# A reordered last stage: output norms on four column tiles, normalised input turned by DMA

## The chip, the cores and the metric

The kernel runs on one core of one Trainium2 chip. The metric is the device time of one launch in microseconds (us), as the median over runs. The engines are named as in the profile: PE (TensorE matmul), PEld (its weight loads), DVE (VectorE), ACT (ScalarE), POOL (GpSimd) and SP (SyncE, which issues most DMAs here).

## The reference, cut to what matters

The model has two layers, each an attention and a feed-forward part, over 16 batches of 256 tokens of width 256. The last part is a gated linear attention. For one batch, `x` being 256 by 256:

```python
xn = layernorm(x)
q1, k1, v = xn @ Wq, xn @ Wk, xn @ Wv          # 8 heads of 64
q2 = xn @ Wqa @ Wqb;  k2 = softmax(xn @ Wka @ Wkb)
gk1, gk2 = log_sigmoid(xn @ Wg1a @ Wg1b) / 16, log_sigmoid(xn @ Wg2a @ Wg2b) / 16
e = softmax(xn @ We);  mask = one_hot(top1(e));  fac = e * mask
o = gla(q1, k1, v, gk1) + sum over experts of gla(q2*fac, k2*fac, v, gk2*mask)
g = xn @ Wga @ Wgb
o = o * rsqrt(mean(o*o over the head's 64 columns) + eps) * norm_w
o = o * (g * sigmoid(g))
x = x + tanh(g_ffn) * (o @ Wo)
```

The change touches how this part is scheduled and, most of all, the line with `rsqrt(mean(o*o))`, which this text calls the output norm: one factor for each token and head, 256 by 8 for a batch.

## The kernel before, in words

The kernel computes everything in float32. Stages 0 to 2 hold the first three parts of the model. The last stage (`stage3_fast`) takes up about the last third of the span and is written as a software pipeline by hand.

The stage's loop `for p in range(last)` runs over 64 steps: `p // 4` is the batch and `p % 4` a pair of heads, so a batch has four steps. A pair's data lie with the 128 columns of two heads over the partitions and the 256 tokens along the free dimension. In every step the same core work is done for one pair:

- `keys_queries(p+1)`: keys and queries of the next step into the PSUM bank `kq` (four 128x256 products).
- `decays(p+1)`: cumulated gate logarithms for the dense part (`gq`, with the mask `dmask`) and the routed part (`gz`, with the mask `em`); ACT makes `ee`, their exponentials.
- `products(p, 0)`: attention scores of the dense part into the PSUM tile `sc`. There is one such tile of two banks, so the next user of `sc` waits until VectorE has read it.
- `masked(p, 0)`: VectorE multiplies `sc` with a mask into `at`. `factors(p+1)`: VectorE makes `f` from `kq` and `ee`.
- `values(p-1)`: `at` of the step before times `v`, into the PSUM bank `o`.
- `second(p+1)`, `factors_second(p+1)`: second half of `gq`, and keys of the routed part for a later batch (`e2`); VectorE makes `q`, POOL makes `k`.
- `products(p, 1)`: scores of the routed part, again into `sc`; in the next step `masked(p, 1)` has VectorE multiply them (four instructions), and POOL add them to `at`.

The rest of a batch's work is hung into these steps by tables (`start`, `copies`, `middle`, `rest`, `late`, `behind_mask`, `by_rows`, `logs`): each maps `p % 4` to a list of functions with a distance in batches. The engines keep the order in which the program issues instructions, each engine for itself, so these tables fix the queues of PE, VectorE, ACT, POOL and SP. The functions that the change and the prediction touch:

- `stats`, `norm_ahead`: mean and variance of `x` (VectorE, then four small POOL instructions), and the normalised `xn` (two ACT instructions), two batches ahead.
- `turn_ahead`: `xn` is turned into `xnT` with 16 VectorE transposes of 32 partitions by 128 columns (a 128-column instruction turns four blocks of 32x32).
- `lows`: PE multiplies `xnT` with the low-rank matrices; VectorE copies them to `low`, and a second time 2x32 rows to `low2`; a DMA makes `lowd`.
- `outgates`: PE makes the gate logits `zg` in two banks; ACT makes `eg = exp(-zg)` and copies `zg` to `zs`.
- `all_gates`: gate logits `z` in two banks, and in the same tile `sc` that the scores use.
- `route`, `turn_hot`, `turned_hot`, `pairs`: the chosen expert of each token, its transpose `hT`, and the masks `em` and `am` from it (`both`).
- `shares`, `shares_end`: softmax denominators of the second keys on four column tiles (`den`: four 32x256 products, each with 32 of the 128 columns of PE), a VectorE transpose and their running maximum `second`.
- `squares`, `gated`, `scaled`, `project`: the squares of `o` (`sq`), `u = o * gate`, the output norm (`ms`: a 128x512 product with the block matrix `halves` for each two pairs, which puts each head's sum on all of its 64 partitions; ACT takes logarithm and exponential into `r`; POOL multiplies), and the output projection.

The VectorE instruction order of `shares_end` and `outgates` matters for what follows, since `masked(p, 1)` comes behind them in the queue.

Of the kernel before, what the change touches and what calls it, by code (L numbers as in the profile page):

```python
# [10 lines left out]
F32 = mybir.dt.float32  # L11
I32 = mybir.dt.int32
AF = mybir.ActivationFunctionType
ALU = mybir.AluOpType
AX = mybir.AxisListType
PSUM = bass.MemoryType.PSUM

P = 128
B, S, D = 16, 256, 256
# [4 lines left out]
V_LN1G, V_LN1B, V_LN2G, V_LN2B, V_QB, V_KB, V_NW, V_ONE, V_GATE, V_N = 0, 2, 4, 6, 8, 10, 12, 13, 14, 18  # L24


def bc(ap, shape, *axes):

    for a in axes:
        ap = ap.unsqueeze(a)  # L30
    return ap.to_broadcast(list(shape))
# [42 lines left out]
def layers(ctx: ExitStack, tc: tile.TileContext, t, out, check):  # L74
    nc = tc.nc
# [10 lines left out]
    xs, cs = [None] * B, [None] * B  # L86
# [132 lines left out]
    def normed(dst, src, mv, rs, p=P, n=2):  # L219
        for i in range(n):  # L220
            act.activation(dst[:, i, :], src[:, i, :], AF.Identity, bias=rs[:p, 1, i:i + 1],
                           scale=rs[:p, 0, i:i + 1])

    def turned_squares(xT, x, portion):

        for n in portion:
            q, r = n // 4 * 32, n % 4 * 32
            dve.transpose(xT[r:r + 32].rearrange("p k (i s) -> p i k s", i=2)[:, :, :, q:q + 32],
                          x[q:q + 32].rearrange("p i (k d) -> p i k d", k=2)[:, :, :, r:r + 32])
# [1389 lines left out]
    def stage3_fast(early_bank):  # L1619

        with ExitStack() as sx:
# [7 lines left out]
            def bank(name):  # L1629
                return pss.tile([P, 512], F32, tag="ps", name=name) if pss else early_bank(name)  # L1630
# [5 lines left out]
            def matmul(*a, **k):  # L1636
                tc.keep_in_program_order(nc.tensor.matmul(*a, **k))  # L1637
# [33 lines left out]

            def norm_ahead(b):
                xn[b] = w0.tile([P, 2, D], F32, tag="xn", name="xn")
                normed(xn[b], xs[b], *mvs.pop(b))

            def turn(b):
                xnT[b] = of(b).tile([P, 2, S], F32, tag="xnT", name="xnT")
# [6 lines left out]
            def turn_ahead(b):  # L1684

                xnT[b] = of(b).tile([P, 2, S], F32, tag="xnT", name="xnT")
                turned_squares(xnT[b], xn[b], range(16))

            def lows(b):

                low[b] = of(b).tile([P, 2, S], F32, tag="low", name="low")
                ps = bank("low")
                for c in range(2):
                    for k in range(2):
                        matmul(ps[:, c * S:(c + 1) * S], la[:, k, c * P:(c + 1) * P], xnT[b][:, k, :],
                                         start=k == 0, stop=k == 1)
                dve3.tensor_copy(low[b][:, 0, :], ps[:, :S])
                dve3.tensor_scalar(low[b][:, 1, :], ps[:, S:], vec[:, V_ONE:V_ONE + 1], None, ALU.add)
                lowd[b] = of(b).tile([P, S], F32, tag="lowd", name="lowd")
                nc.sync.dma_start(out=lowd[b][64:], in_=low[b][:64, 1, :])  # L1700
                if b > 0:
                    for r in range(0, 64, 32):
                        dve3.tensor_scalar(low2[r:r + 32, :], ps[64 + r:96 + r, S + P:],
                                           vec[64 + r:96 + r, V_ONE:V_ONE + 1], None, ALU.add)

            e_, den_, z_ = {}, {}, {}

# [99 lines left out]
            def outgates(b):  # L1807

                gw[b] = w2.tile([P, 4, S], F32, tag="gw", name="gw")
                two = [bank("zg"), bank("zg")]  # L1810
                for i in range(2):
                    for h, (w, x) in enumerate(((lbg[0:64], low[b][0:64, 1, :]), (lbg2[64:], lowd[b][64:]))):
                        m = 2 * i + h
                        matmul(two[h][:, i * S:(i + 1) * S], w[:, m * P:(m + 1) * P], x, start=True, stop=True)
                for h, ps in enumerate(two):
                    e, zs = (w2.tile([P, 512], F32, tag=n, name=n) for n in ("eg", "zs"))
                    act3.activation(e, ps, AF.Exp, scale=-1.0)
                    act3.copy(zs, ps)
                    z_[b, h] = zs, e

            def outgates_end(b, h):
# [55 lines left out]
            def shares_end(b):  # L1877
                ps = z_.pop((b, "den"))
                den = w2.tile([P, 8, 32], F32, tag="dens", name="dens")
                dve3.transpose(den.rearrange("p x j -> p (x j)"), ps[:, :S])  # L1880
                rd[b] = st.tile([P, 8, 2], F32, tag="kden", name="kden")
                flat = rd[b].rearrange("p x j -> p (x j)")
                most = check["second"].rearrange("p (x j) -> p x j", j=2)
                dve3.tensor_tensor(most, most, den[:, :, 0::16], ALU.max)
                dve3.reciprocal(rd[b], den[:, :, 0::16])
                pool3.tensor_tensor(check["rsum"][:, :16], check["rsum"][:, :16], flat, ALU.add)

# [62 lines left out]
            def squares(b, mp):  # L1950
                if mp == 0:
                    u_[b] = w2.tile([P, 4, S], F32, tag="u", name="u")
                    oT[b] = w2.tile([P, 4, S], F32, tag="oT", name="oT")
                ps = o.pop((b, mp))
                sq[b, mp] = w2.tile([P, 512], F32, tag="sq", name="sq")
                act3.activation(sq[b, mp], ps, AF.Square)
                z_[b, mp, "o"] = ps

            def gated(b, mp):
# [3 lines left out]

            def scaled(b, mp, by=pool3, beside=()):
                ps = bank("ms")
                matmul(ps, halves, sq.pop((b, mp)), start=True, stop=True)
                for x in beside:
                    x()
                r = w2.tile([P, 512], F32, tag="r", name="r")
                act3.activation(r, ps, AF.Ln, bias=eps, scale=1.0 / 64,  # L1970
                                     accum_out=check["logs"][:, 2 * b + mp:2 * b + mp + 1])
                act3.activation(r, r, AF.Exp, scale=-0.5)
                by.tensor_tensor(oT[b][:, 2 * mp:2 * mp + 2, :].rearrange("p m s -> p (m s)"),
                                        u_[b][:, 2 * mp:2 * mp + 2, :].rearrange("p m s -> p (m s)"), r, ALU.mult)

            def project(b):
                ps = bank("proj")
# [25 lines left out]
                    matmul(ps, ones, v[B - 1][:, 0, :], start=True, stop=True)  # L2003


            start = {2: [(turn_hot, 1)]}
            copies = {2: [(turned_hot, 1)]}
            middle = {0: [(lows, 1)], 1: [(all_gates, 1)], 2: [(pairs, 1)], 3: [(scaled, 0, 0)]}

            rest = {0: [(bias, 2)], 1: [(route, 1)], 2: [(steepest, 1, 0), (stats, 2)], 3: [(steepest, 1, 1), (turn_ahead, 2)]}  # L2010
            late = {1: [(scaled, -1, 1)], 2: [(project, -1)], 3: [(vals, 1)]}
            behind_mask = {0: [(route_logits, 1)]}
            by_rows = {0: [(outgates, 0)], 1: [(gates_end, 1)]}
            logs = {0: [(route_sums, 1), (outgates_end, 0, 0)], 1: [(outgates_end, 0, 1), (gate_logs, 1, 0)], 2: [(gate_logs, 1, 1), (norm_ahead, 2)]}

            def run(steps, p):
                for f, d, *a in steps.get(p % 4, ()):
                    if 0 <= p // 4 + d < B:
                        f(p // 4 + d, *a)
# [36 lines left out]
            for p in range(last):  # L2056
                if p == 0:
                    turn(1)
                run(start, p)
                if p % 4 == 0:  # L2060
                    shares(p // 4)
                if 0 < p:
                    masked(p - 1, 1)
                run(copies, p)
                if p % 4 == 0:
                    shares_end(p // 4)
                if 1 < p and p % 2 == 1:
                    gated((p - 2) // 4, (p - 2) % 4 // 2)
                if p + 1 < last:
                    keys_queries(p + 1)  # L2070
                run(middle, p)
                run(rest, p)
                if p + 1 < last:
                    decays(p + 1)
                run(late, p)
                products(p, 0)
                masked(p, 0)
                run(behind_mask, p)
                if p + 1 < last:
                    factors(p + 1)  # L2080
                run(by_rows, p)

                inside = p % 4 > 0 and p + 1 < last
                if inside:
                    summed(p)
                if p + 1 < last:
                    second(p + 1)
                    factors_second(p + 1)
                run(logs, p)
                products(p, 1)  # L2090
                if 0 < p and not inside:
                    summed(p)
# [128 lines left out]
```

## Time and profile before

| | us |
|---|---|
| median of 3 runs | 1845.09 |
| the three runs | 1840.51, 1845.09, 1845.21 |
| the profiled execution | 1847.08 |
| span of its profile | 1845.3 |
| mean granted TensorE clock in it | 0.995 |
| one batch of the last stage in its steady state (from one `v` product group to the next) | 37.72 |

The profiled execution took 1.8 us more than the span from its first to its last instruction, and 2.0 us more than the median of the runs. A row of the timeline has the start and the duration in us, the engine, the line (that of a helper for most instructions here, so rows are told apart by their tiles), the operation, the tile written, the tile read, the shape, how many instructions the row merges, and in brackets how long the engine had been idle and who released it. A float32 product appears as two instructions. Matmul ends are modelled, so distances between starts are more to be trusted than durations.

### The profile page before, as it was taken

Reading aid. Unit: us, or ns where it says so; the run is one execution under the profiler, and the core shown is the slowest. Engines: PE = TensorE matmul, PEld = TensorE weight load, DVE = VectorE, ACT = ScalarE, POOL = GpSimd, SP = SyncE. Lnnn points to the kernel's source line nnn. Section 1 sums busy time; section 2 is a strip of 40 time slices with the busy share of each in tenths; the row PEclk is TensorE's granted clock in tenths of the full one; section 3 lists DMA queues with packets and bytes.
Section 4 is the critical chain, followed back from the end, with each engine's and each line's share of the span. In section 5 each row is a group of like instructions: output and inputs, shape, how many; then the busy total and the mean of one; then the engine's idle time right before and its main releaser. Section 6 shows DMA issues by size and latency. Waiting matters only on the chain.

```text
span 1845.3 us, 35182 instructions
## 1 busy us (share of the span) xinstructions
PE 1813.5 (98%) x13870; PEld 1249.8 (68%) x13870; DVE 1231.5 (67%) x2903; ACT 873.9 (47%) x1804; POOL 1017.0 (55%) x1001
## 2 busy tenths in 40 slices
PE   8999999999999999999999999999999999999997
PEld 5666666666766667666777766656767777777765
DVE  3355656566665666656474488867888878878874
ACT  4433344433444334443433487846555645455543
POOL 4654767567676576756634767315444444444433
PEclk9999999999999999999999999999999999999999
DMA  9800010000010100000077933100000000000000
GB/s 304 226 1 22 16 34 15 25 17 23 23 37 8 29 19 10 31 23 18 13 248 238 233 49 49 18 4 3 14 8 10 8 10 13 8 9 8 14 9 14
DMA packets 68504, 85.86 MB, mean 47 GB/s; under 512 B 10740, under 2 KB 55908, under 8 KB 67818
## 3 DMA queue, kind: packets, MB, share of 16 engines
q1 hardware_dynamic: 56041, 66.74, 11.5%
q0 software_dynamic: 12288, 16.79, 4.5%
q8 instruction: 111, 1.82, 0.4%
q14 instruction: 64, 0.52, 0.1%
HBM read 44.17 MB, written 38.29 MB: 45 GB/s over the span
## 4 chain that ended last, share of the span: by engine, by line
PE 82%; POOL 9%; DVE 4%; issue 2%; ACT 2%; DMA 1%; SPq 0%; POOLq 0%; DVEq 0%; ACTq 0%
PE o L50 11%; PE qk L50 11%; PE v L50 8%; PE sc L50 8%; PE proj L50 7%; PE kq L1637 7%; PE sc L1637 5%; POOL es L50 4%; PE gq L1637 3%; PE v L1637 3%; PE o L1637 3%; PE proj L1637 3%; POOL x L50 2%; PE ex L50 2%; POOL rs L50 2%
## 5 line engine op out<-in xcount | busy, mean ns | idle before, releaser
L50 POOL TENSOR_SCALAR rs<-mv 128x2 f32<-128x2 f32 (+2 forms) x85 | 16.3, 192 | 376.8 <-DVE mv L50 371.1
L50 DVE RECIPROCAL rd<-o 128x256 f32<-128x256 f32 x64 | 112.3, 1755 | 164.0 <-PE o L50 123.7
L50 POOL TENSOR_TENSOR at<-at,at 128x768 f32<-128x768 f32 x63 | 114.1, 1812 | 142.4 <-DVE at L50 142.4
L50 ACT ACTIVATE e<-sc 128x1024 f32<-128x1024 f32 (+1 forms) x192 | 181.7, 1016 | 18.4 <-PE sc L50 18.4
L50 PE MATMUL sc<-qk 64*128 64x256 f32 (+1 forms) x1536 | 183.1, 384 | 0.5 <-DVE qk L50 0.5
L50 PE MATMUL o<-e,v 128*32 128x256 f32 (+1 forms) x3072 | 177.9, 379 | 0.0
L50 PEld LDWEIGHTS sc<-qk 64*128 64x128 f32 (+1 forms) x1536 | 132.0, 172 | 55.1 <-issue 26.8
L50 POOL TENSOR_TENSOR esum<-esum,es 128x512 f32<-128x512 f32 x128 | 163.5, 1277 | 10.0
L50 PE MATMUL qk<-kvT,wkv 128*128 128x333 f32 x512 | 164.3, 443 | 0.0
L50 ACT ACTIVATE qk<-qk 128x256 f32<-128x256 f32 x128 | 48.8, 381 | 231.4 <-PE qk L50 231.4
L50 POOL TENSOR_TENSOR es<-e 128x1024 f32<-128x1024 f32 x64 | 151.2, 2363 | 12.1 <-ACT e L50 9.0
L50 POOL TENSOR_TENSOR es<-es,e 77x1024 f32<-77x1024 f32 x64 | 150.4, 2350 | 5.0
L50 PEld LDWEIGHTS o<-e,v 128*32 128x32 f32 (+1 forms) x3072 | 99.9, 110 | 66.3
L50 PE MATMUL qk<-kvT,wq 128*128 128x256 f32 x512 | 134.6, 385 | 0.0
L50 DVE COPY qk<-qk 128x333 f32<-128x333 f32 x128 | 64.6, 504 | 93.8 <-ACT qk L50 92.8
L50 POOL DMA_INDIRECT x<-rows_out,pos x64 | 101.1, 1580 | 33.2 <-issue 17.0
L50 PEld LDWEIGHTS qk<-kvT,wq 128*128 128x128 f32 x512 | 94.3, 189 | 35.2 <-issue 9.6
L50 PEld LDWEIGHTS qk<-kvT,wkv 128*128 128x128 f32 x512 | 97.2, 190 | 30.0
L50 PE MATMUL proj<-wo0h,oT 128*128 128x256 f32 x512 | 113.7, 380 | 0.3 <-DVE oT L50 0.3
L50 PE MATMUL v<-wkv,kvT 128*128 128x512 f32 x256 | 113.1, 595 | 0.0
L50 PEld LDWEIGHTS proj<-wo0h,oT 128*128 128x128 f32 x512 | 95.9, 190 | 13.9 <-issue 0.8
L50 POOL DMA_INDIRECT rows<-xw,pos x64 | 66.8, 1043 | 61.1 <-ACT xT L50 24.0
(265 smaller groups left out, 4085.7 us busy)
## 6 DMA issues: line engine op xcount, KB each, us to landing
rows<-zero SPq DMA_DIRECT2D x16, 640.0 KB
xin<-rows SPq DMA_DIRECT2D x16, 640.0 KB
rows_out<-y SPq DMA_DIRECT2D x16, 384.0 KB
v<-vctx SPq DMA_DIRECT2D x15, 308.0 KB
x<-in_x_dram SPq DMA_DIRECT2D x16, 256.0 KB
rows_out<-y SPq DMA_DIRECT2D x16, 256.0 KB
out_dram<-x SPq DMA_DIRECT2D x15, 256.0 KB
wkv<-in_wkv_dram SPq DMA_DIRECT2D x2, 1024.0 KB
```

The costliest lines, as they stand in the source:

```text
L50: x = getattr(self.engine, name)(*a, **k)
L1637: tc.keep_in_program_order(nc.tensor.matmul(*a, **k))
```

## The change

It does the following in the last stage, for all batches but the last where the output norm is concerned:

- The output norm of a batch is done at once (`norms`) instead of in two halves: four 32x256 products on four column tiles, one for each pair, with 32 columns of `halves`; then one logarithm and one exponential over 128x256; the eight useful rows go to DRAM, and two DMAs bring them back, each row spread over the 64 partitions of its head. POOL's two multiplications (`normed_out`) are later, and in place, as `oT` is now the same tile as `u`.
- `turn_ahead` has one VectorE transpose of 128x512 into a new tile `turned` (32x32 blocks in place), and 16 DMAs on SP's queue, each 32 partitions by 4 pieces of 128 bytes, put the blocks where they belong. `norm_ahead` writes `xn` in an order that suits this.
- `low2` is made by a DMA from `low` in place of two VectorE instructions.
- `outgates`: VectorE copies `zg` to `zs`, where ACT did.
- `shares_end`: the running maximum is a reduction with one operand into a column of its own, where it was a `max` of two tiles.
- The tables are changed, and in the first step of a batch `values` comes before `second`, as in the other three.

```diff
             def norm_ahead(b):
...
-                normed(xn[b], xs[b], *mvs.pop(b))
+                every = "p i (k d) -> p i k d"
+                normed(xn[b].rearrange("p k (i d) -> p i k d", i=2), xs[b].rearrange(every, k=2), *mvs.pop(b))
             def turn_ahead(b):
...
-                turned_squares(xnT[b], xn[b], range(16))
+                y = w1.tile([P, 4, P], F32, tag="turned", name="turned")
+                dve3.transpose(y.rearrange("p x d -> p (x d)"), xn[b].rearrange("p k d -> p (k d)"))
+                to = xnT[b].rearrange("p k (i s) -> p (k i) s", i=2)
+                for q in range(0, P, 32):
+                    for r in range(0, P, 32):
+                        nc.sync.dma_start(out=to[r:r + 32, :, q:q + 32], in_=y[q:q + 32, :, r:r + 32])
             def lows(b):
...
-                    for r in range(0, 64, 32):
-                        dve3.tensor_scalar(low2[r:r + 32, :], ps[64 + r:96 + r, S + P:],
-                                           vec[64 + r:96 + r, V_ONE:V_ONE + 1], None, ALU.add)
+                    nc.sync.dma_start(out=low2, in_=low[b][64:, 1, P:])
             def outgates(b):
...
-                    act3.copy(zs, ps)
+                    dve3.tensor_copy(zs, ps)
             def shares_end(b):
...
-                most = check["second"].rearrange("p (x j) -> p x j", j=2)
-                dve3.tensor_tensor(most, most, den[:, :, 0::16], ALU.max)
+                dve3.tensor_reduce(check["second"][:, b:b + 1], den[:, :, 0::16], AX.XY, ALU.max)
...
+            rms = [tc.dram_tile([8, S], F32, name=f"rms{b}") for b in range(B - 1)]
+            def scaled_first(b):
+                if b == B - 1:
+                    scaled(b, 0)
+            def norms(b):
+                if b == B - 1:
+                    return
+                ps, x = bank("ms"), sq.pop(b)
+                for m in range(4):
+                    matmul(ps[32 * m:32 * m + 32, :S], halves[:, 48:80], x[:, m, :], start=True, stop=True)
+                y = w2.tile([P, S], F32, tag="rs", name="rs")
+                act3.activation(y, ps[:, :S], AF.Ln, bias=eps, scale=1.0 / 64, accum_out=check["logs"][:, 2 * b:2 * b + 1])
+                act3.activation(y, y, AF.Exp, scale=-0.5)
+                nc.sync.dma_start(out=rms[b], in_=y[0:P:16, :])
+                r = z_[b, "r"] = w1.tile([P, 4, S], F32, tag="r", name="r")
+                for j in range(2):
+                    nc.sync.dma_start(out=r[64 * j:64 * j + 64],
+                                      in_=bc(rms[b].rearrange("(m j) s -> j m s", j=2)[j], [64, 4, S], 0))
+            def normed_out(b, mp):
+                if b < B - 1:
+                    x, r = oT[b][:, 2 * mp:2 * mp + 2, :], z_[b, "r"][:, 2 * mp:2 * mp + 2, :]
+                    pool3.tensor_tensor(x, x, r, ALU.mult)
...
-            start = {2: [(turn_hot, 1)]}
-            copies = {2: [(turned_hot, 1)]}
-            middle = {0: [(lows, 1)], 1: [(all_gates, 1)], 2: [(pairs, 1)], 3: [(scaled, 0, 0)]}
-            rest = {0: [(bias, 2)], 1: [(route, 1)], 2: [(steepest, 1, 0), (stats, 2)], 3: [(steepest, 1, 1), (turn_ahead, 2)]}
-            late = {1: [(scaled, -1, 1)], 2: [(project, -1)], 3: [(vals, 1)]}
+            start = {3: [(pairs, 1)]}
+            middle = {0: [(lows, 1)], 1: [(all_gates, 1)], 2: [(turn_hot, 1)], 3: [(scaled_first, 0)]}
+            rest = {0: [(bias, 2)], 2: [(turned_hot, 1), (norm_ahead, 2)], 3: [(steepest, 1, 0), (steepest, 1, 1)]}
+            late = {1: [(norms, -1)], 2: [(vals, 1)], 3: [(project, -1)]}
...
-            logs = {0: [(route_sums, 1), (outgates_end, 0, 0)], 1: [(outgates_end, 0, 1), (gate_logs, 1, 0)], 2: [(gate_logs, 1, 1), (norm_ahead, 2)]}
+            logs = {0: [(route_sums, 1), (outgates_end, 0, 0)],
+                    1: [(route, 1), (stats, 2), (outgates_end, 0, 1), (gate_logs, 1, 0)],
+                    2: [(gate_logs, 1, 1), (turn_ahead, 2), (normed_out, -1, 0), (normed_out, -1, 1)]}
...
-                run(copies, p)
...
-                inside = p % 4 > 0 and p + 1 < last
+                inside = 0 < p and p + 1 < last
```

More of the change, by code (lines that the diff above doesn't have):

```diff
@@ L1952, in squares @@
                     u_[b] = w2.tile([P, 4, S], F32, tag="u", name="u")
-                    oT[b] = w2.tile([P, 4, S], F32, tag="oT", name="oT")
+                    oT[b] = u_[b]
+                    sq[b] = w2.tile([P, 4, S], F32, tag="sq", name="sq")
                 ps = o.pop((b, mp))
-                sq[b, mp] = w2.tile([P, 512], F32, tag="sq", name="sq")
-                act3.activation(sq[b, mp], ps, AF.Square)
+                act3.activation(sq[b][:, 2 * mp:2 * mp + 2, :].rearrange("p m s -> p (m s)"), ps, AF.Square)
                 z_[b, mp, "o"] = ps
@@ L1965, in scaled @@
                 ps = bank("ms")
-                matmul(ps, halves, sq.pop((b, mp)), start=True, stop=True)
+                matmul(ps, halves, sq[b][:, 2 * mp:2 * mp + 2, :].rearrange("p m s -> p (m s)"), start=True, stop=True)
                 for x in beside:
                     x()
-                r = w2.tile([P, 512], F32, tag="r", name="r")
+                r = w1.tile([P, 4, S], F32, tag="r", name="r")[:, :2, :].rearrange("p m s -> p (m s)")
                 act3.activation(r, ps, AF.Ln, bias=eps, scale=1.0 / 64,
```

## The prediction

> **What bounds the kernel now.** I read the page first, then the busy time of two batches of the last stage, then its timeline, engine by engine.
>
> ```profile
> PE 1813.5 (98%) x13870; PEld 1249.8 (68%) x13870; DVE 1231.5 (67%) x2903; ACT 873.9 (47%) x1804; POOL 1017.0 (55%) x1001
> ...
> 1489.31:1527.02 37.71, 37.51 (x245) 27.11 (x245) 30.74 (x75) 20.21 (x47) 17.80 (x18) 1.00 0.03 10
> 1527.02:1564.74 37.72, 37.51 (x246) 27.12 (x245) 30.73 (x75) 20.22 (x47) 17.79 (x18) 1.00 0.03 10
> ```
>
> The second and third lines are two batches, one each: the stretch, its length, busy time of PE, PEld, DVE, ACT and POOL, the granted clock, the DMA share. PE is taken for 37.5 of 37.7 us at full clock; VectorE has 7 us free, ACT and POOL over 17. So a batch costs what PE's queue costs, and work taken off VectorE or ACT is worth only the PE stalls that it causes. Some are hidden, since busy PE includes modelled ends. I therefore take the distance from one start to the next as a "slot". PE's timeline, batch by steps 0 to 3:
>
> ```profile
> 1501.02 0.76 PE L1637 MATMUL sc<-f 64*128 64x256 f32 x6
> ...
> 1503.37 0.92 PE L1637 MATMUL sc<-q,k 64*128 64x256 f32 x8 [0.19 <-DVE e L50]
> ...
> 1506.97 0.70 PE L1637 MATMUL sc<-lbg,low 17*128 17x512 f32 x2
> ...
> 1508.02 0.71 PE L1637 MATMUL gq<-dmask,lg 128*128 128x128 f32 x4
> ...
> 1509.02 1.02 PE L1637 MATMUL ms<-sq,halves 128*128 128x512 f32 x2
> 1509.97 0.92 PE L1637 MATMUL sc<-f 64*128 64x256 f32 x8
> ...
> 1525.11 1.02 PE L1637 MATMUL ms<-sq,halves 128*128 128x512 f32 x2
> 1525.97 0.61 PE L1637 MATMUL gq<-dmask,lg 128*128 128x128 f32 x4
> ...
> 1533.36 0.64 PE L1637 MATMUL den<-e,halves 128*32 128x256 f32 x8
> 1533.93 1.13 PE L1637 MATMUL kq<-xnT,wk 128*128 128x256 f32 x4
> ```
>
> The two `ms` have slots of 0.95 and 0.86 us. `den`, the shape of the new norms, has 0.57 us for four products, so the column tiles overlap. Before `sc<-q,k` of step 0 there is a stall of 0.46: its predecessor `gq/gz` starts at 1502.48 and needs 0.43. VectorE in the same stretch:
>
> ```profile
> 1502.00 0.96 DVE L50 TENSOR_TENSOR at<-sc,amask 128x768 f32<-128x768 f32 x1 [0.46 <-PE sc L1637]
> ...
> 1503.14 0.68 DVE L50 TENSOR_TENSOR f<-kq,ee 128x512 f32<-128x512 f32 x1
> 1503.74 0.41 DVE L50 TENSOR_TENSOR q<-gq,ee 128x256 f32<-128x256 f32 x1
> ...
> 1504.34 1.39 DVE L50 SCALAR_TENSOR_TENSOR at<-sc,kden,am 128x256 f32<-128x256 f32 x4
> ...
> 1526.43 5.03 DVE L50 STREAM_TRANSPOSE xnT<-xn 32x128 f32<-32x128 f32 x16
> ```
>
> The last row of step 0 frees `sc` at 1505.73; `all_gates`, which writes `sc`, is reached by PE at 1506.97, so there are 1.2 us of reserve.
>
> **The change, part by part.**
>
> **1. Norms on column tiles.** Out of PE's queue go 0.95 + 0.86 = 1.81 us a batch; in come four 32x256 products, 0.57 by the row of `den`. Gain: 1.24. Since PE is the bound, it counts in full, unless a later wait takes it back. The factors' way is long: ACT's logarithm and exponential over 256 columns (0.4 + 0.2 + 0.4, half the columns of the 0.69 and 0.63 now), a store of eight rows, then two loads of 256 KB that wait for the store. The lowd DMA is issued at 1500.86, and the trace has its last landing at 1502.73: 1.9 us. So 0.4 + 1.9 for the store, 0.9 + 1.9 plus about 0.8 of transfer for the loads: about 7 us from PE's product, ACT's queue of 1 us included. The reader is POOL's `normed_out`, 11 us later in POOL's queue (behind `k` of step 2). Cover 4 us; were it gone, POOL's addition into `at` behind it would hold PE's `values`. The two multiplications (1.27 each) stand in POOL's idle time before step 3 and end 2.5 us before `project`. In all, the DMA way costs nothing.
>
> **2. Copy to `zs` on VectorE.** It takes 2 x 0.59 off ACT, which is worth nothing, and adds two 128x512 copies out of PSUM to VectorE, between `f` and `q`. No row shows one; `f`, 512 columns, takes 0.68 with 0.60 to its successor, and copies of 256 columns 0.43, so 1.2 for both (bounds 1.1 to 1.4). In the changed program's order each copy also waits for ACT's `eg` of its bank, which costs some 0.25. So `masked(0,1)` ends 1.46 later, at 1507.19 on the old clock. PE, however, gets to `all_gates` sooner, see 3.
>
> **3. `values` before `second` in step 0.** PE fills the 0.46 with a product that is ready (POOL's addition ended at 1499.05). PE then reaches `all_gates` at about 1506.45 and stands until 1507.25 for `sc`. Its first two products go ahead, on other rows of PE; the second two end at about 1508.15 against 1508.02 now. So 2 and 3 together cost 0.1 us (bounds -0.5, if the copies are quick and the 0.46 stays won, to +0.5).
>
> **4. Turning by DMA.** 5.03 us of VectorE become one transpose: 32x128 takes 0.30, 128x256 0.44, so 128x512 about 0.7. Worth nothing by itself, as those 5 us lay under `v` and 16 are now DMAs on SP, that `lows` waits for. Time for them: from VectorE's transpose behind `q` of step 2 to `lows`, PE has both 0.85, kq 1.83, gq/gz 1.0, proj 3.55, sc 0.85, o 0.80, gq/gz 0.54, sc 0.78, den 0.57, kq 1.83: 12.6, less 0.7 for the transpose, 11.9 us. Needed: 15 distances of issue and 1.9 for the last landing. SP's queue in stage 1:
>
> ```profile
> 927.51 0.38 SPq L1110 DMA_DIRECT2D cT<-in_ctxT_dram  x1
> 927.93 0.42 SPq L1107 DMA_DIRECT2D mk<-in_maskT_dram  x1
> 928.39 0.38 SPq L1110 DMA_DIRECT2D cT<-in_ctxT_dram  x1
> 928.82 0.42 SPq L1107 DMA_DIRECT2D mk<-in_maskT_dram  x1
> ...
> 938.06 3.10 SPq L1110 DMA_DIRECT2D cT<-in_ctxT_dram  x4
> ```
>
> `cT` is the nearest row (256 pieces of 308 bytes): 0.45 apart in the good case, 3.10/4 = 0.78 in the worse. At 0.47 the last lands after 15 x 0.47 + 1.9 = 9.0, with 2.9 to spare: cost nothing; I take this, as nothing else is then on SP. At 0.78 it is 13.6, 1.7 late. [...] The rows show issues 0.45 apart, so the latency is paid once; I follow the rows. Nothing queues behind on SP but the output store, and `lowd`, which comes after `lows` anyway. The `low2` DMA follows `lowd` (landing 2.4 us after `low`, read 5 us after it).
>
> **5. The maximum `second`** takes 1.54 us as POOL's addition runs, against 0.19 at best. [...] Moved to the end of step 1, `route` meets an idle POOL (it waits for `stats` behind it) and takes 1.45. `turn_hot` needs it about 0.4 later; with one such block there PE would lose 1.1.
>
> **6. Moved steps.** `norm_ahead` now precedes ACT's `ee` in step 2 and waits for POOL's four, they for `stats`: `ee` ends some 3 us later than it could, 2 us before `factors(3)` needs it. POOL's order there is `rs`, `gw`, addition: the addition ends about 0.4 before `values(1)` needs it. `pairs` ahead of step 3 feeds `em` 1.8 us before `gz`. `project` in step 3 covers `masked(2,1)` and its followers as it did in step 2. All these cost nothing by this count; the last is the tightest, bounds 0 to 0.5. At the very end `project` falls into the last step's stalls: 0.45 and 1.22 for `sc`, gain 0 to 0.6.
>
> **The sum.** 1.24 - 0.1 = 1.1 us (rounded) for each of 15 batches: 16.5. The profiled execution took 1847.1, so 1830.6; it stood 2.0 above the median, so the forecast is 1829 (1828.6). What a measurement can tell from no change is 0.3%, 5.5 us.
>
> **The rivals.**
> - *The turn comes late (slower).* The place is PE's `low` in step 0; from a distance of (11.9 - 1.9)/15 = 0.67 us between issues on, PE stands there, 15 us more for each us above it, 14 times. At 0.78 that is 1.7 x 14 = 23 against 16.5: 1851. At 1.0 it would be 1898. For it: 16 issues in a row are found nowhere in the stage, the pieces are of 128 bytes. Against: 256 pieces went at 0.45.
> - *VectorE takes the gain back (no change).* The 1.1 are lost again if step 0's chain of VectorE is 1.1 longer than counted, or POOL's addition misses `values(1)`: 1845.
> - *The stalls go too (more gain).* With 2 and 3 at -0.5, 1.74 x 15 = 26: 1819.
> - That the norms' four products don't overlap: four slots of 0.46 (a quarter of `kq`'s 1.83), so nothing won; `den` speaks against it. Counted with no change.
>
> **How the numbers follow.** Forecast with its near variants 0.56, more gain 0.12, so faster 0.68; no change 0.12; slower 0.20, nearly all by the turn. The likeliest case's own range is 1822 to 1838. The range 1819 to 1851 takes in the extra gain, no change and the mild turn; left out are the turn at 0.8 or more and unforeseen gains.
>
> **What would show it.** Right: batch period about 36.6; slot of `ms` about 0.57, once a batch; a `sc<-lbg` row that waits for DVE by up to 0.8; no wait for `low` beyond 0.1. Wrong: PE idle before `low`, released by a DMA or SP; distances of the 16 issues above 0.67; PE idle before `values`, released by POOL; `eq` over 1 us; or a period of 37.7 and more.

## The result, and the profile after

| | us |
|---|---|
| kernel before, median of 20 runs | 1843.30 (1840.51 to 1846.48) |
| changed kernel, median of 20 runs | 1836.04 (1832.85 to 1841.56) |
| ratio | 0.9962, 95% interval 0.9954 to 0.9969 |
| profiled execution of the changed kernel | 1836.71, span 1834.8 |

The change makes the kernel 7 us faster. The forecast was 16.5 us faster: the sign is right, and less than half of the gain arrived.

The page of the changed kernel, and busy time in two of its batches (columns as before: stretch, length, PE, PEld, VectorE, ACT, POOL, granted clock, DMA share, GB/s):

```profile
PE 1802.7 (98%) x13930; PEld 1246.4 (68%) x13930; DVE 1138.6 (62%) x2695; ACT 832.4 (45%) x1727; POOL 1014.3 (55%) x1001
...
1531.77:1568.55 36.78, 36.76 (x249) 26.88 (x249) 24.07 (x59) 17.55 (x41) 17.33 (x19) 1.00 0.13 29
1568.55:1605.29 36.74, 36.72 (x249) 26.99 (x249) 24.06 (x59) 17.54 (x41) 17.62 (x19) 1.00 0.14 32
```

PE still bounds the stage, and VectorE has 12.7 us free in a batch where it had 7. These are two of the best batches, about 0.95 us shorter than before. Measured from the first `low` of one batch to the first `low` of the next, the kernel before has 37.72 nearly always. The changed kernel has anything from 36.74 to 37.37, behind slower batches at the start. Its queue is the same every time, so something comes late irregularly. PE's waits between 1250 and 1830 us of the profile say what (in all, how often, longest, in us):

```profile
PE low L1637 <- DMA xnT<-turned: 3.7, 4, 2.6
```

This view counts only four of the waits (it leaves out short ones); the distance from the `kq` products to `low` shows smaller ones too. It is 1.83 in every steady batch of the kernel before, where `low` is in time, and in the changed kernel it is 1.84 to 2.44 in most batches. The first batch that is turned by DMA is the worst, here PE's and SP's timeline:

```profile
1266.85 1.13 PE L1637 MATMUL kq<-xnT,wk 128*128 128x256 f32 x4
1267.82 1.03 PE L1637 MATMUL kq<-xnT,wq 128*128 128x256 f32 x4
1271.46 3.60 PE L1637 MATMUL low<-xnT,la 128*128 128x256 f32 x8 [2.61 <-DMA xnT<-turned]
```

```profile
1556.77 10.32 SPq L1693 DMA_DIRECT2D xnT<-turned  x16
```

In the first fence `low` begins 4.61 us behind the first `kq`, 2.78 more than its 1.83. Its eight products then take 3.4 us to the next product instead of 1.73. The row of SP is the turn of a later batch: 16 issues in 10.32 us. One takes 0.60, and they begin 0.645 us apart; the last is issued at 1566.50 and has landed at 1568.35, 1.9 us later.

Step 0 and 1 of the same kernel, on PE and then on VectorE, and last one row of the kernel before:

```profile
1540.49 0.70 PE L1637 MATMUL z<-lbg,low 17*128 17x512 f32 x2
1541.01 0.70 PE L1637 MATMUL sc<-lbg,low 17*128 17x512 f32 x2
1541.02 0.59 PE L1637 MATMUL z<-lbg,low 17*128 17x512 f32 x2
1541.55 0.59 PE L1637 MATMUL sc<-lbg,low 17*128 17x512 f32 x2
1542.07 0.71 PE L1637 MATMUL gq<-dmask,lg 128*128 128x128 f32 x4
1542.62 0.61 PE L1637 MATMUL gz<-em,lg 128*128 128x128 f32 x4
1543.16 0.64 PE L1637 MATMUL ms<-sq,halves 128*32 128x256 f32 x8
1543.73 0.92 PE L1637 MATMUL sc<-f 64*128 64x256 f32 x8
```

```profile
1537.78 1.29 DVE L50 COPY zs<-zg 128x512 f32<-128x512 f32 x2 [0.16 <-ACT eg L50]
...
1539.59 1.37 DVE L50 SCALAR_TENSOR_TENSOR at<-sc,kden,am 128x256 f32<-128x256 f32 x4
```

```profile
1506.95 0.70 PE L1637 MATMUL z<-lbg,low 17*128 17x512 f32 x2
```

The norms: one `ms` with a slot of 0.57 (1543.16 to 1543.73), where there were two with 0.95 and 0.86. `all_gates`: `z` starts at 1540.49, its partner `sc` only at 1541.01, since VectorE, behind its two new copies to `zs`, frees `sc` at 1540.96 (1539.59 + 1.37). Before, the pairs ran side by side (`z` at 1506.95, `sc` at 1506.97). So `z` to `gq` takes 1.58 us, where it took 1.07.

Where the 7 us come from, by the batch distances of the two profiles: 12 batches of the steady state give 8.8 us, the rest of the span behind the last `low` 2.1; the three batches at the start lose 1.4, 2.5 and 0.7. That sums to -6.3. The spans differ by 10.5, but 4.2 of it lies ahead of the first `low`, where the two programs do the same work; it is scatter of the two executions. The 1.4 lost in the first batch is scatter too: the same PE rows ran at a granted clock of 0.64 for 9.4 us there. This first distance is 32.73 us in the kernel before, with the clock at half for 3.41 us of it, and 34.12 in the changed kernel, with 6.83 at half. In the twelve profiles of this text it lies between 31.1 and 35.9, and follows none of the edits.

### The profile page after: what moved, and what is told of

Its sections match the earlier page's. It is cut to its first block, busy times and chain, and to the rows that moved or that the text cites. A ratio compares the mean times of both kernels' runs of the same rounds, so it can differ in the third digit from the quotient of the medians.

```text
span 1834.8 us, 35411 instructions
## 1 busy us (share of the span) xinstructions
PE 1802.7 (98%) x13930; PEld 1246.4 (68%) x13930; DVE 1138.6 (62%) x2695; ACT 832.4 (45%) x1727; POOL 1014.3 (55%) x1001
## 3 DMA queue, kind: packets, MB, share of 16 engines
q8 instruction: 112, 1.84, 0.4%
## 4 chain that ended last, share of the span: by engine, by line
PE 84%; POOL 7%; DVE 3%; issue 2%; ACT 2%; SPq 1%; DMA 1%; POOLq 0%; ACTq 0%; DVEq 0%
PE o L50 11%; PE qk L50 11%; PE v L50 9%; PE sc L50 8%; PE proj L50 7%; PE kq L1637 6%; PE sc L1637 6%; PE gq L1637 4%; POOL es L50 4%; PE ex L50 3%; PE v L1637 3%; PE o L1637 3%; PE proj L1637 2%; PE low L1637 2%; PE gz L1637 2%
## 5 line engine op out<-in xcount | busy, mean ns | idle before, releaser
L50 DVE TENSOR_TENSOR at<-sc,amask 128x768 f32<-128x768 f32 x64 | 61.2, 957 | 133.7 <-PE sc L1637 78.2
L50 POOL DMA_INDIRECT x<-rows_out,pos x64 | 100.9, 1577 | 35.6 <-issue 16.5
```

The costliest lines, as they stand in the source:

```text
L50: x = getattr(self.engine, name)(*a, **k)
```

## The experiments

My theory behind the result: the norms' gain is real; the 16 DMAs give most of the missing part back, as they come late at `low`, and VectorE's copies give back the rest at `all_gates`. Each edit below is to the changed kernel unless it says otherwise. Ratios are to the kernel before.

**The turn begun earlier.** VectorE's transpose waits for nothing but `xn`, which ACT had ready at 1551.6; VectorE took it up at 1556.0, behind `q`.

```diff
-            late = {1: [(norms, -1)], 2: [(vals, 1)], 3: [(project, -1)]}
+            late = {1: [(norms, -1)], 2: [(vals, 1), (turn_ahead, 2)], 3: [(project, -1)]}
...
-                    2: [(gate_logs, 1, 1), (turn_ahead, 2), (normed_out, -1, 0), (normed_out, -1, 1)]}
+                    2: [(gate_logs, 1, 1), (normed_out, -1, 0), (normed_out, -1, 1)]}
```

> The changed kernel with one step moved: the turn (VectorE's transpose and its 16 DMAs) is called behind the products for v in step 2 and no longer behind the q of that step, where xn has been ready for some 4 us. Theory A (the 16 DMAs are what the gain was given back to: 0.645 us apart they take 15 x 0.645 + 1.9 = 11.6 us against 11.9, so low waits now and then, and by 2 us and more in the first turned batch): with 4 us more of time no low waits; from the last k,q product to low 1.83 us in every batch, the sum of the waits comes back, 5 to 7.5 us: about 1829 to 1831, ratio to the kernel before 0.992 to 0.993. Rival B (the turn's lateness is small change, the loss lies in step 0 and 1 on VectorE): within 2 us of the changed kernel, ratio 0.995 to 0.997. Rival C (VectorE's earlier transpose waits for xn and holds up the factors of step 3): slower than the changed kernel, ratio above 0.997.

Measured: 1827.36 us, ratio 0.9916 (0.9902 to 0.9931). Theory A, and slightly more than its 5 to 7.5 us. From `kq` to `low` there are 1.83 us in every batch, the first turned one included, which had 4.61:

```profile
1265.10 1.13 PE L1637 MATMUL kq<-xnT,wk 128*128 128x256 f32 x4
1266.07 1.03 PE L1637 MATMUL kq<-xnT,wq 128*128 128x256 f32 x4
1266.93 1.89 PE L1637 MATMUL low<-xnT,la 128*128 128x256 f32 x8
```

The batch distance is 36.69 or 36.70 in all but one of the twelve. SP's row of one batch and the busy times of another:

```profile
1544.65 11.59 SPq L1693 DMA_DIRECT2D xnT<-turned  x16
```

```profile
1524.11:1560.80 36.69, 36.67 (x249) 26.95 (x248) 24.14 (x59) 17.57 (x41) 17.65 (x19) 1.00 0.14 33
```

The issues are no quicker (0.644 us apart; in this batch one of them took 1.86 and made the 16 last 11.59), they only begin 4.4 us sooner. Of such a slip nothing reaches PE. This one move is worth 8.7 us by the medians, more than the whole change.

**`zs` back on ScalarE.**

```diff
-                    dve3.tensor_copy(zs, ps)
+                    act3.copy(zs, ps)
```

> The changed kernel with the two copies to zs back on ScalarE. Theory A2 (the two copies, 0.685 us each and a wait for eg before them, are what makes the second pair of all_gates wait 0.5 us for its tile): masked of step 0 ends about 1.5 us sooner, the z and sc rows run side by side again, the step from z to gq falls from 1.58 to about 1.07: 15 x 0.5 = 7.5 us less, ratio 0.992. Rival B2: the banks of zg are then freed by ScalarE later and z waits for ScalarE instead, or the 0.5 turns up at the next VectorE wait: ratio 0.995 to 0.997 as in the changed kernel.

Measured: 1832.63 us, ratio 0.9936 (0.9921 to 0.9952): between the two theories. The wait at `all_gates` is gone as A2 said, but half of it comes back 3 us later:

```profile
1533.71 0.70 PE L1637 MATMUL z<-lbg,low 17*128 17x512 f32 x2
1533.72 0.70 PE L1637 MATMUL sc<-lbg,low 17*128 17x512 f32 x2
...
1537.56 0.65 PE L1637 MATMUL o<-at,v 128*64 128x256 f32 x4 [0.19 <-POOL at L50]
```

`z` and `sc` start together again. But ACT now has 1.2 us more ahead of `eg`'s last form, POOL's `gw` waits for that, POOL's addition into `at` stands behind `gw`, and PE's `values` of step 1 comes 0.27 late for it. Net 0.24 a batch, about 3.4 us. (The medians differ by 3.4 too, but the six runs lie between 1826.7 and 1834.7, so the rows are the firmer evidence.) This is the forecast's "POOL's addition misses `values(1)`", met from the other side.

**`values` behind `second` again.**

```diff
-                inside = 0 < p and p + 1 < last
+                inside = p % 4 > 0 and p + 1 < last
```

> The changed kernel with values behind second again in step 0 (the old place). By the count behind the forecast the 0.46 us stall in front of sc<-q,k returns, and the wait of about 0.5 us at all_gates goes, since TensorE gets there later: within 1.5 us of the changed kernel, ratio 0.9955 to 0.997. Rival: the product of values in the new place costs 0.2 us more than in the old one (the slot from zg to o is 0.30 and was 0.09) beyond the stall that it fills, so the old place is better: 3 us less, ratio 0.9945. The other rival: the new place keeps its 0.46 and the wait at all_gates stays: 5 to 7 us more, ratio 0.999 to 1.000.

Measured: 1836.18 us, ratio 0.9959 (0.9946 to 0.9972). No difference from the changed kernel in time, as counted, but not quite by the count: `z` to `gq` falls from 1.58 to 1.33 and not to 1.07. The old place loses 0.25 in step 0 and PE stands 0.25 less at `all_gates`.

**The norms alone, on the kernel before.** `squares`, `scaled`, `scaled_first`, `norms` and `normed_out` are those of the changed kernel; the tables get what these need.

```diff
-            middle = {..., 3: [(scaled, 0, 0)]}
+            middle = {..., 3: [(scaled_first, 0)]}
-            late = {1: [(scaled, -1, 1)], 2: [(project, -1)], 3: [(vals, 1)]}
+            late = {1: [(norms, -1)], 2: [(vals, 1)], 3: [(project, -1)]}
-            2: [(gate_logs, 1, 1), (norm_ahead, 2)]
+            2: [(gate_logs, 1, 1), (norm_ahead, 2), (normed_out, -1, 0), (normed_out, -1, 1)]
```

> The kernel before with the norms part alone: norms on four column tiles, factors by way of DRAM, the products into the output in place, and the places that this needs (project behind the decays of step 3, vals in step 2). The turn stays 16 transposes on VectorE, zs on ScalarE, values behind second, second by a two-input maximum. Theory A (1.24 us a batch of TensorE's queue is a real gain, and the other parts of the change gave back about half): 15 x 1.15 to 1.24 = 17 to 19 us less than before, ratio 0.990 to 0.991. Rival D (column tiles are worth less in place than their rows show, the other parts gave nothing back): ratio 0.995 to 0.997, as the whole change. Rival E (project in step 3 stands on transposes of 5 us on VectorE that v used to cover): ratio 0.998 or more.

Measured: 1854.19 us, ratio 1.0065 (1.005 to 1.008), 11 us slower than before. Theory A falls in the form in which it stood there, rival E holds. The `ms` slot is 0.57 here too, so the 1.24 is won, and more than lost. VectorE's and PE's timeline in step 3:

```profile
1569.09 5.04 DVE L50 STREAM_TRANSPOSE xnT<-xn 32x128 f32<-32x128 f32 x16
1574.16 0.75 DVE L50 SCALAR_TENSOR_TENSOR x<-proj,gate,x 128x512 f32<-128x512 f32 x1
1574.82 0.95 DVE L50 TENSOR_TENSOR at<-sc,amask 128x768 f32<-128x768 f32 x1
```

```profile
1575.83 0.92 PE L1637 MATMUL sc<-q,k 64*128 64x256 f32 x8 [1.26 <-DVE at L50]
```

With the new norms, `project` must wait until step 3, and its addition on VectorE (0.75) comes into the step that has the 16 transposes (5.04). `masked`, which frees `sc`, is behind both, and PE stands. The slot ahead of `sc<-q,k` is 1.64, and 0.21 where it doesn't wait: 1.43 lost. A further 0.43 goes in step 1; the experiment on `route` below is on that.

**Four DMAs more.** To take the slope; the four write a tile that nothing reads.

```diff
+                spare = w1.tile([P, 4, 32], F32, tag="spare", name="spare")
+                for r in range(0, P, 32):
+                    nc.sync.dma_start(out=spare[r:r + 32], in_=y[0:32, :, r:r + 32])
                 for q in range(0, P, 32):
```

> The changed kernel with four more DMAs of the same size and form in front of the 16 (from VectorE's transpose to a tile that nothing reads), to take the slope. Theory A (each issue costs 0.645 us on SP's queue, and low waits for the last landing): the 16 begin 2.58 us later, and that arrives at low nearly whole: 14 x 2.5 = 35 us more than the changed kernel, about 1871, ratio 1.013 to 1.017; if the granted clock falls after each such wait, as it did once in the changed kernel behind a wait of 2.6 us (low took 3.43 for 1.73), up to 14 x 1.7 = 24 more, ratio up to 1.030. Rival B (the issues are not what low waits for): within 5 us of the changed kernel, ratio 0.995 to 0.999.

Measured: 1895.34 us, ratio 1.0291 (1.0276 to 1.0306): theory A, with a granted clock of 0.96 from 1300 to 1700 us, where the changed kernel has 1.00. 59 us over 14 batches are 4.2 us for 2.58 us of issues. PE's timeline in one batch, and the busy times of the stretch in which its `low` runs (the eighth column is the granted clock):

```profile
1555.75 1.03 PE L1637 MATMUL kq<-xnT,wq 128*128 128x256 f32 x4
1559.43 3.45 PE L1637 MATMUL low<-xnT,la 128*128 128x256 f32 x8 [2.66 <-DMA xnT<-turned]
```

```profile
1559.40:1562.70 3.30, 3.27 (x9) 2.64 (x10) 0.00 (x0) 0.00 (x0) 0.00 (x0) 0.55 0.09 30
```

`low` begins 4.65 us behind the first `kq` (1554.78) and so 2.8 late, and then runs at a clock of 0.55, so that it takes 3.24 to the next product and not 1.73. A late transfer is paid twice here.

**Early turn, and `zs` on ScalarE.** Both former edits.

> Both former edits on the changed kernel: the turn called behind the products for v, and both copies to zs on ScalarE. If the two causes are separate, the batch period is 36.69 (early turn) less 0.51 at all_gates plus the 0.27 that the ScalarE copies cost at POOL's addition ahead of values of step 1: 36.45, some 3.4 us less than the early turn alone: about 1824, ratio 0.9895 to 0.9905. If they were one cause seen twice: no better than the early turn, ratio 0.991 to 0.9925.

Measured: 1822.47 us, ratio 0.9896 (0.9882 to 0.9911); the batch distance is 36.43 (36.45 expected). The two causes are separate, and add.

**Early turn, and one copy to `zs` on each engine.**

```diff
-                    dve3.tensor_copy(zs, ps)
+                    (act3.copy if h else dve3.tensor_copy)(zs, ps)
```

> The early turn, with one of the two copies to zs on VectorE (the first) and one on ScalarE (the second). Theory: VectorE then ends masked of step 0 some 0.7 us sooner, enough to take away the 0.51 at all_gates; ScalarE has 0.59 more rather than 1.18, so that POOL's gw and the addition behind it end in time for values of step 1 (with both copies on ScalarE they were 0.27 late). Batch period 36.69 - 0.51 = 36.18: 15 x 0.5 = 7.5 us under the early turn: about 1820, ratio 0.987 to 0.988. Rival: the 0.27 at POOL's addition comes with the first 0.59 already: about 1824, ratio 0.9895 to 0.9905. Other rival: masked of step 0 is still late: ratio 0.9915.

Measured: 1818.10 us (1817.83 to 1818.36), ratio 0.9867 (0.9853 to 0.9881). This is the best version, 25 us faster than the kernel before and 18 faster than the change. In the steady state PE waits for nothing that the profile shows, and every batch takes the same:

```profile
1519.33:1555.51 36.18, 36.16 (x249) 26.67 (x248) 23.55 (x58) 18.00 (x42) 17.70 (x19) 1.00 0.14 33
```

**Norms and early turn on the kernel before.** The norms as above, and the turn by DMA (new `norm_ahead` and `turn_ahead`), to see whether these two are the pair that belongs together.

```diff
-            rest = {0: [(bias, 2)], 1: [(route, 1)], 2: [(steepest, 1, 0), (stats, 2)], 3: [(steepest, 1, 1), (turn_ahead, 2)]}
+            rest = {0: [(bias, 2)], 1: [(route, 1)], 2: [(steepest, 1, 0), (norm_ahead, 2)], 3: [(steepest, 1, 1)]}
+            late = {1: [(norms, -1)], 2: [(vals, 1), (turn_ahead, 2)], 3: [(project, -1)]}
-            logs = {..., 1: [(outgates_end, 0, 1), (gate_logs, 1, 0)], 2: [(gate_logs, 1, 1), (norm_ahead, 2), ...]}
+            logs = {..., 1: [(outgates_end, 0, 1), (gate_logs, 1, 0), (stats, 2)], 2: [(gate_logs, 1, 1), ...]}
```

> The kernel before with two parts: the norms (as in the run of that part alone), and the turn by 16 DMAs, begun early behind the products for v; stats at the end of step 1 and norm_ahead in step 2, as the early turn needs. zs on ScalarE, values behind second in step 0, second by a two-input maximum, turn_hot, pairs and route in their old places. Theory A (norms alone lost 12 us instead of gaining 18 because the 5.04 us of transposes on VectorE, with project's addition behind them, no longer fit under project: the stall of 1.43 ahead of sc<-q,k in step 3; the turn by DMA is what makes the room): the stall is gone, batch period 36.6 to 37.0, ratio 0.990 to 0.994. Rival (the loss of norms alone lies in the norms: mode changes, the DRAM way, products in place): still slower than before, ratio above 1.000.

Measured: 1838.63 us (22 runs), ratio 0.9977 (0.997 to 0.9983). Faster than before, but by 4 us where 11 to 18 were expected. The stall of 1.43 ahead of `sc<-q,k` in step 3 is gone, so this part of the theory holds. The batch distance is 37.54 all the same: step 1 has the slot of 0.55 (for 0.21) ahead of `sc<-q,k`, and PE waits for `hT`, which VectorE copies behind its late work:

```profile
1547.04 0.89 PE L1637 MATMUL both<-hT 4*128 4x256 f32 x4 [0.53 <-DVE hT L50]
```

The second half of `kq` before it starts at 1545.48, so its slot is 1.56; in the kernel before it is 0.96. The next experiment is on the first of the two; the second was not taken further.

**`route` back ahead of the decays of step 1,** in the best version.

```diff
-            rest = {0: [(bias, 2)], 2: ...
+            rest = {0: [(bias, 2)], 1: [(route, 1)], 2: ...
-                    1: [(route, 1), (stats, 2), ...
+                    1: [(stats, 2), ...
```

> The early turn with one zs copy on each engine, and route called again ahead of the decays in step 1 (its place in the kernel before). There POOL's addition runs beside its eq, which took 1.55 us for 0.17 in the run with norms and turn alone, and masked of step 1 came 0.43 us late for sc<-q,k. If that place is what cost 0.43 in that run: 15 x 0.43 = 6.5 us more than the version with route at the end of the step: about 1824.5, ratio 0.990 to 0.991, eq near 1.5 us. If the loss there had to do with something else (pairs and turn_hot in their old places): 1818, ratio 0.9865.

Measured: 1828.07 us, ratio 0.9925 (0.9912 to 0.9939), 10 us more than the best version; batch distance 36.82 for 36.18. The instructions that write or read `eq` (minimum, median and maximum in ns):

```profile
L50 DVE TENSOR_TENSOR eq<-e,em x16: 166/1546/1550, 1220.1 to 1759.7; 128x8 f32<-128x8 f32 x16
```

1.55 us for 128x8 elements, where the changed kernel's `eq` takes 0.17. In the kernel before, where `route` has this place, it ends as POOL's addition ends (1510.02 and 1510.00):

```profile
1508.17 1.83 POOL L50 TENSOR_TENSOR at<-at,at 128x768 f32<-128x768 f32 x1
...
1508.47 1.55 DVE L50 TENSOR_TENSOR eq<-e,em 128x8 f32<-128x8 f32 x1
```

In the run `masked` of step 1 is then late, and the slots around `sc<-q,k` are 0.75 and 0.85 where they are 0.21 and 0.75. That is 0.64 a batch. The move of `route`, counted as nothing in the forecast, is what lets the norms' gain through in step 1.

**The two-input maximum for `second` back,** in the best version.

```diff
-                dve3.tensor_reduce(check["second"][:, b:b + 1], den[:, :, 0::16], AX.XY, ALU.max)
+                most = check["second"].rearrange("p (x j) -> p x j", j=2)
+                dve3.tensor_tensor(most, most, den[:, :, 0::16], ALU.max)
```

> The early turn with one zs copy on each engine, and the maximum for second again with two inputs (1.54 us beside POOL's addition in the kernel before, 0.18 with one input). The forecast called this edit worth nothing. In the version without it VectorE idles 2.08 us behind second and kden until TensorE's low; 1.35 us more still fit: same time as that version, 1818, ratio 0.9855 to 0.988. Rival (the long maximum is what pushed the copies of low, or masked of step 0): 15 x 0.6 us or more, ratio above 0.991.

Measured: 1820.51 us, ratio 0.9882 (0.9867 to 0.9897). The batch distance is 36.18 again, to the hundredth, though the instruction takes 1.6 us for 0.18. The median stands 2.4 us higher, a hair above the expected range, but the intervals of the two versions overlap, and the profiles differ by 1.6 us in the first distance (32.73 for 31.09), the one that scatters. So the edit is worth nothing in the steady state, as in the forecast's sum, which has no term for it:

```profile
L50 DVE TENSOR_TENSOR second<-second,dens x16: 186/1602/1608, 1233.3 to 1773.4; 128x16 f32<-128x16 f32 x16
```

## Why the prediction was wrong, and what in it was right

The sign was right, and what the norms give was right. The size was wrong, 7 us for 16.5, and the step that failed is part 4: the turn by DMA was put at no cost, with 2.9 us to spare, and it cost about 8.7. By the parts of the forecast:

1. *Norms, gain of 1.24.* Right. The slot is 0.57 in every version, and the factors' way by DRAM does not show in the steady batches: POOL's `normed_out` starts without a wait. But that way was longer than counted: each load landed 3.7 to 4.3 us after its issue, the whole took about 9 us and not 7, and 2 us of cover are left of the 4. The 0.8 of transfer counted for the loads was an estimate that no row shows. A small loss was not counted: `gz` to `ms` takes 0.54 where it took 0.45.
2. *Copies to `zs`.* The durations were right (0.685 each, and 0.16 of wait for `eg`).
3. *`values` first.* Right in kind: PE stands at `all_gates`. Parts 2 and 3 together cost 0.25 a batch, not 0.1: 0.51 is lost at `all_gates`, and of the stall of 0.46 only 0.25 stays won, since from the last `zg` product to the next group there are now 0.31 (to `o`, 1536.17 to 1536.48) where there were 0.10 (to `gq`, 1502.38 to 1502.48). The best version shows the rest of the term: with one copy moved back, the 0.51 returns and the two parts win 0.25. That is half of the bound of -0.5.
4. *The turn costs nothing.* This is the step that failed, by its size: the mechanism (PE stands at `low` when the last DMA lands late) was in the forecast. Two terms were wrong. The distance between issues was taken from the good case of `cT`, 0.47; it is 0.645. So 15 x 0.645 + 1.9 = 11.6 of 11.9 us are needed, and the "2.9 to spare" are 0.3, which every small slip of one issue uses up. And the 11.9 held 3.55 of `project`, which in the first turned batch has no batch before it to project: there `low` was 2.8 late. The forecast named the threshold (0.67) and the place, but gave the passage up to it no price. By the early turn, 8.7 us went here. Of these, 8.1 can be read from the profile of the changed kernel: 2.8 of wait in the first turned batch and 1.7 by the lower clock behind it, which the forecast did not have at all, 2.8 in the small waits of the other batches, and 0.8 because `low` takes about 1.80 and not 1.73 to its successor in them.
5. *`second` worth nothing.* Right: the sum has no term for it, and in the best version, where VectorE idles 2.08 us behind it and `kden` for PE's `low`, the batch distance is 36.18 with either form.
6. *Moved steps cost nothing.* Right, and they even win a little: `gq` of step 2, now behind `hT` and not behind `both`, has a slot of 0.45 for 0.55, and that ahead of `den` is 0.75 for 0.78, together 0.13 a batch. (The DMA for `low2` and the moves of `pairs` and `turn_hot` were not run alone.) That `route`'s move gains was missed: it is worth 0.64 a batch once the norms no longer cover the wait. So was that the transposes on VectorE can't stay once `project` is in step 3: "worth nothing by itself" is true of the old order only. The parts are worth their gain only together: the norms alone are 11 us slower than before, with the early turn 4 faster, and with the rest of the change 16 faster.

The sum, term by term: -16.5 forecast; +8.7 for the turn, 15 x 0.15 = +2.2 for parts 2 and 3, 15 x 0.09 = +1.4 for `gz` to `ms`, 15 x 0.13 = -2.0 for the moved steps. That gives -6.2, against -7 measured, whose interval is 5.7 to 8.5 us. The 8.7 is itself known only to within some 3 us, so that the sum closes this well is partly luck.

Of the rivals, the late turn came to pass below its threshold, and took about half of the gain; it would have had to take twice that to make the kernel slower. With the turn in time the measured 1827.4 lies 1.6 under the forecast's 1829, at a batch distance of 36.69 against 36.6. That is luck in part: the uncounted 0.15 and 0.09 and the uncounted gain of 0.13 nearly cancel.

## What to carry to other kernels

A chain of small transfers with a deadline is priced with the distance of the very form that it uses, and with the first round of the pipeline, where the cover may be missing; if the spare time is less than the doubt in one distance times the number of transfers, begin it earlier before anything else. When work is taken out of the bounding engine's queue, look for what that work was covering: the next latest wait (here `route`, the transposes, `all_gates`) takes the gain. And put a copy that two engines could do on the one whose followers are not awaited next, splitting it if both are tight.

## What the runs showed of the hardware

- An issue of 32 partitions by 4 pieces of 128 bytes, SBUF to SBUF, took 0.60 us of SP's queue (the median of 224 in the changed kernel), 0.645 from one to the next; in the good rows of stage 1 of the kernel before, the issues of `cT` and `mk` were 0.42 to 0.46 apart. The longest of the 224 took 1.33, and one in the run with the early turn 1.86. The landing, 1.9 us, was paid once and not 16 times, as the forecast had followed from the rows: the first of 16 was issued at 1556.77, the last at 1566.50, and that one had landed at 1568.35.
- A wait of PE can cost more than its length. In the changed kernel the granted clock fell to half for 3.41 us behind the wait of 2.61:

```profile
1267.95:1271.36 3.41, 0.90 (x5) 0.44 (x3) 0.54 (x3) 0.00 (x0) 3.19 (x3) 1.00 0.13 22
1271.36:1274.77 3.41, 3.31 (x8) 2.72 (x9) 0.00 (x0) 0.00 (x0) 0.00 (x0) 0.50 0.02 5
1274.77:1278.20 3.43, 3.41 (x32) 2.79 (x32) 1.86 (x5) 1.21 (x4) 0.73 (x1) 1.00 0.13 29
```

  These are the busy times of the changed kernel up to the fall, during it and behind it; the clock is the third number from the right. In the first stretch PE was busy for 0.90 us and so idle for 2.5. In the run with 20 DMAs `low`, behind a wait of 2.66, ran at a clock of 0.55 from 1559.40 to 1562.70 and took 3.24 us to the next product. In the run with `zs` on ScalarE the wait ahead of `low` in the first turned batch was 2.64, but the clock was 1.00 from 1263.00 to 1272.00, and `low` took 1.80 to the next product. So about the same wait may or may not cost some 1.7 us more. In the traces of the kernel before and of the changed one the changes of the clock in the span are whole multiples of 3.413 us apart (in the changed kernel 6.83, 37.55, 3.41 and 552.96 us: 2, 11, 1 and 162 of them). Whether a wait costs more by where it falls among these multiples, no run here shows. The clock also fell where PE had been idle for less: in the kernel before at 1213.23, with 1.15 us idle in the 3.41 ahead of it, and in the changed kernel at 1226.98, with 0.67; why stays open.
